# A transformer layer on one core: closing stores taken one to a step, an empty item before the token slots, and a last sum one step later

## The chip, the cores and the metric

The kernel runs on one core of a Trainium2 chip. The metric is the device time of one execution in microseconds (us). A core has TensorE (PE, matrix products, with its weight loads PEld), VectorE (DVE), ScalarE (ACT), GpSimd (POOL) and SyncE (SP). Each engine works through its own instructions in order; SyncE and POOL issue the transfers (DMA) between the chip's main memory (HBM) and the core's memory. Products land in PSUM, of which the kernel holds seven tiles of 512 columns for general use (`unit()`) and an eighth for attention sums.

## What is computed

Four sequences of 1024 tokens with 256 channels go through an attention block and a mixture-of-experts block. All is float32.

```python
x = hidden_states                                   # 4 x 1024 x 256
x = x + layernorm(attention(layernorm(x)))          # 16 heads of 16
    # scores = (q k' + c2p + p2c) / sqrt(48), where c2p and p2c are looked up
    # in products with 128 relative positions by the distance of query and key;
    # out = layernorm(softmax(scores) v Wo + bo + input) * scale + bias
y = layernorm(x)
e = argmax(softmax(y Wr + br))                      # one of 8 experts a token
out = sum over i of (relu((y where e == i) W1[i] + b1[i]) W2[i] + b2[i])
x = x + layernorm(out)
```

A token that is not expert i's enters it as zeros and still receives `relu(b1[i]) W2[i] + b2[i]`. These constants are summed once into one row for each expert, the row of "the other experts" (`drow`, stored to `dh`), and added to the output of the token's own expert.

## The kernel before

**Steps.** The attention works through 128 steps `u` (4 batches x 4 groups of four heads x 8 tiles of 128 queries), and four more that only finish. In step `u`, `tables(u + 4)` multiplies queries and keys with the position tables (L470), copies the result (L478) and stores it to HBM (`shift`, L484). `skewed` reads it back so that each row is shifted by one against the row before it (L497), once as `kpos` and once as `qpos`; it reads for step `u + 3` (`kpos`) and `u + 2` (`qpos`). `mend` (L504, VectorE) adds what lies beyond the table's end: in step `u` for the `kpos` that was issued in step `u - 1`, and for a `qpos` likewise. `turn_x` (L535) brings `kpos` into PSUM, `first_x` (L551) adds the scores, `near_x` (L567, L571) adds `qpos` and takes maxima. `first_y` (L584, L591) does the rest of the keys. A block of four steps later, `turn_near` (L620) and `second` (L642) build the transposed scores, `Exp` (L649) is taken and `attend` (L659) sums. `divide` (L678 to L683) ends a block of four steps, in the first step of the next four.

**Closing work.** When `divide` ends the last group of a batch, it calls `finish` for that half of the batch (first half: steps 32, 64, 96, 128; second half: four steps later). `finish` does nothing at once: it puts items in `queue`. Each step takes items at fixed places (`slot()`, one item each). A step takes three: steps that are not a multiple of four take one ahead of `turn_x`, one ahead of the tables and one at the end, after `first_y`; steps that are a multiple of four take one behind `divide`, one ahead of the tables and one ahead of `first_y`. In the four steps after 127 and in the loop over expert blocks there are five places. The items of a half, with two tile pairs `t` = 0 and 2 each:

- `turn` (L744, L746): transposes; `out_proj` (L754, L758): the product with Wo, the residual, first statistics
- `scale` (L767, L768); then one item of its own, `fetch(b, hf, "x")`, two loads (L727)
- `scaled`, `residual` (POOL, L780), `again`: two further norms; then, for first halves, one item `fetch(b, 1, "xrh")`, two loads (L727) of the second half's residual
- `logits0` (`xn`), `logits` (L806), `logits2` (L817), interleaved: the routing logits
- `choose`: four stores (L785), for each pair one to `x1h` and, but for the last batch, one to `x1a`; then thirteen VectorE instructions (L833 to L843) that find each token's expert and count
- `place` (L849, L850 on TensorE, then VectorE): each token's slot in its expert's list. L849 needs what L840 wrote, L850 what the last L842 wrote
- an item that puts four `scatter` (L862, POOL) in the list `late`, of which `one_late()` takes one in each step

In the step numbers, before the change: `choose` of batch 0's first half stands in the last place of step 38 and `place` in the first of step 39; of its second half in the first and second place of step 46. The other batches follow 32 steps apart each.

**The row of the other experts.** From step 6 on, `others(e)` loads an expert's W2 and `others2(e)` multiplies (L708) and adds to `dsum` (L711, VectorE). In step 29, with the last expert, L714 multiplies with `dsum` right behind L711, L715 adds to `drow` and L716 stores it.

**Expert blocks.** After step 127, 39 blocks of up to 128 tokens are worked through, each with its expert's weights (2 MB). The first 17 hold only tokens of batches 0 to 2 and begin while batch 3 is being finished; their order in `queue` is guarded by `late` being empty. The lists of tokens (`lists`) are first filled with a pad value in step 7 (L226 to L228).

Of the kernel before, what the change touches and what calls it, by code (L numbers as in the profile page):

```python
# [15 lines left out]
P = 128  # L16
B, S, C = 4, 1024, 256
# [7 lines left out]
E, FF = 8, 1024  # L25
# [17 lines left out]
SLOTS = E * NTOK + NTOK  # L43
I32 = mybir.dt.int32
# [4 lines left out]
def tile_layer(  # L49
# [7 lines left out]
    nc = tc.nc  # L57
# [13 lines left out]
    lists = hbm.tile([SLOTS, 1], I32, name="lists")  # L71
# [10 lines left out]
    def rsqrt(agg, n, eps):  # L82

        ve = small.tile([P, NT], F32, name="ve")
        rs = small.tile([P, NT], F32, name="rs")
        nc.vector.tensor_scalar(ve[:, :n], agg[:, :n, 1], eps, None, ALU.add)  # L86
        nc.gpsimd.tensor_tensor(rs[:, :n], ve[:, :n], half[:, :n], ALU.pow)  # L87
        return rs
# [10 lines left out]
    with ExitStack() as ax:  # L99
# [16 lines left out]
        xrh = dram.tile([NTOK, C], F32, name="xrh")  # L116
# [3 lines left out]
        def unit():  # L120
            return p_u.tile([P, 512], F32, name="u")
# [90 lines left out]
        def route_setup():  # L212
            nc.vector.tensor_scalar(ebase, iota, float(E), float(NTOK), ALU.add, ALU.mult)
            nc.gpsimd.affine_select(
                out=before, in_=ones_m, pattern=[[1, P]], compare_op=ALU.is_gt, fill=0.0, base=0, channel_multiplier=-1
            )
            nc.gpsimd.iota(ids, pattern=[[P, B * NT]], base=0, channel_multiplier=1)
            nc.gpsimd.memset(count, 0.0)
            nc.gpsimd.memset(dsum, 0.0)
            for e in range(E):  # L220
                nc.vector.tensor_reduce(four[:, e : e + 1], ident[:, e::HP], AX.X, ALU.add)
            nc.vector.tensor_scalar(num_e, iota, float(E), None, ALU.add)
            nc.gpsimd.iota(steps, pattern=[[1, B * NT]], base=0, channel_multiplier=0, allow_small_or_imprecise_dtypes=True)
            nc.vector.tensor_scalar(behind_t, steps, float(TB), None, ALU.mult)
            nc.vector.tensor_scalar(ahead_t, behind_t, float(TB), None, ALU.add)
            pad = blk_p.tile([P, SLOTS // P], I32, name="pad", bufs=1)  # L226
            nc.gpsimd.memset(pad, NTOK)
            nc.sync.dma_start(out=lists.rearrange("(p n) o -> p (n o)", p=P), in_=pad)  # L228


        def others_tiles(sp):
# [172 lines left out]
        blk_p = ax.enter_context(tc.tile_pool(name="blk", bufs=4))  # L404
# [285 lines left out]
        def others(e):  # L690
            w2 = []
            for n in range(2):
                w2.append(ctp.tile([P, NFC // 2, C], F32, name="w2", tag="o", bufs=2))
                nc.sync.dma_start(
                    out=w2[n], in_=w2_d[e, n * FF // 2 : (n + 1) * FF // 2].rearrange("(f p) c -> p f c", p=P)
                )
            lift = small.tile([P, NFC, HP], F32, name="lift", bufs=2)
            nc.vector.memset(lift, 0.0)
            nc.vector.tensor_copy(lift[:, :, :E], rb[:, e * NFC : (e + 1) * NFC].unsqueeze(2).to_broadcast([P, NFC, E]))
            nc.vector.memset(lift[:, :, e : e + 1], 0.0)  # L700
            begun[e] = w2, lift

        def others2(e):
            w2, lift = begun.pop(e)
            pm = unit()
            for f in range(NFC):
                r = f % 4 * HP
                nc.tensor.matmul(  # L708
                    pm[r : r + HP, :C], lhsT=lift[:, f, :], rhs=w2[f // 4][:, f % 4, :], start=(f < 4), stop=(f >= 4)
                )  # L710
            nc.vector.tensor_tensor(dsum, dsum, pm[:, :C], ALU.add)  # L711
            if e == E - 1:
                pm = unit()
                nc.tensor.matmul(pm[:E, :C], lhsT=four, rhs=dsum, start=True, stop=True)  # L714
                nc.vector.tensor_tensor(drow, drow, pm[:E, :C], ALU.add)  # L715
                nc.sync.dma_start(out=dh, in_=drow)  # L716

        queue, late, fetched = [], [], {}

        def fetch(b, hf, what, places=None):  # L720

            for t in range(0, NT // 2, 2):
                if (b, hf, t, what) not in fetched:
                    w = fetched[b, hf, t, what] = places.pop(0) if places else xin.tile([P, 2, C], F32, name="xt")
                    r0 = b * NT + hf * (NT // 2) + t
                    src = xrh.rearrange("(t p) c -> p t c", p=P) if what == "xrh" else x_d.rearrange("b (t p) c -> p (b t) c", p=P)
                    nc.sync.dma_start(out=w, in_=src[:, r0 : r0 + 2, :])  # L727

        def finish(b, hf):


            HT = NT // 2
            t_0 = hf * HT
            ctx_, o = ctxs[b], ctp.tile([P, HT, C], F32, name="o", bufs=2)
            agg = [small.tile([P, HT, 2], F32, name=f"agg{n}", bufs=2) for n in range(3)]
            rs, keep_ = {}, {}
            pairs = range(0, HT, 2)
# [26 lines left out]
            def scale(t):  # L764
                for n in range(t, t + 2):
                    w = o[:, n, :]
                    nc.vector.scalar_tensor_tensor(w, w, agg[0][:, n, 0:1], obb[:, 1, :], ALU.subtract, ALU.mult)  # L767
                    nc.vector.scalar_tensor_tensor(w, w, rs[0][:, n : n + 1], obb[:, 2, :], ALU.mult, ALU.add)  # L768

            def scaled(t):  # L770
                for n in range(2):
# [10 lines left out]
            def store(t):  # L782
                r0 = (b * NT + t_0 + t) * P
                for d in (x1h, x1a) if b < B - 1 else (x1h,):
                    nc.sync.dma_start(out=d[r0 : r0 + 2 * P, :].rearrange("(t p) c -> p t c", p=P), in_=o[:, t : t + 2, :])  # L785

            def again(t):
                for n in range(2):
                    stats(agg[2][:, t + n, :], o[:, t + n, :])
                if t == HT - 2:  # L790
                    rs[2] = rsqrt(agg[2], HT, 1e-5)

            lg = small.tile([P, HT, E], F32, name="lg", bufs=2)

# [31 lines left out]
            acc = small.tile([P, HT, E], F32, name="acc", bufs=2)  # L826

            def choose():
                for t in pairs:
                    store(t)  # L830

                mx = small.tile([P, HT], F32, name="big")
                nc.vector.tensor_reduce(mx, lg, AX.X, ALU.max)  # L833

                io = iota.unsqueeze(1).to_broadcast([P, HT, E])
                nc.vector.tensor_tensor(lg, lg, mx.unsqueeze(2).to_broadcast([P, HT, E]), ALU.is_equal)
                nc.vector.tensor_tensor(lg, lg, io, ALU.mult)
                ix = small.tile([P, HT], F32, name="ix")
                nc.vector.tensor_reduce(ix, lg, AX.X, ALU.min)
                nc.vector.tensor_tensor(lg, io, ix.unsqueeze(2).to_broadcast([P, HT, E]), ALU.is_equal)  # L840
                for t in range(HT):
                    nc.vector.tensor_copy(acc[:, t, :], count)  # L842
                    nc.vector.tensor_tensor(count, count, lg[:, t, :], ALU.add)  # L843
# [27 lines left out]
            for f in (scale, scaled, residual, again):  # L871
                for t in pairs:
                    queue.append((f, t))
                if f is scale:
                    queue.append((fetch, b, hf, "x"))
                if f is again and hf == 0:
                    queue.append((fetch, b, 1, "xrh"))
            for t in pairs:
                queue.append((logits0, t))
                if t:  # L880
# [1 line left out]
                queue.append((logits, t))  # L882
            queue.append((logits2, HT - 2))
            queue.append((choose,))
            queue.append((place,))
            part = b - (B - 2) if hf and b >= B - 2 else None
            plan = [] if part is None else [(need, part), (spread, part), (slots, part)]
# [217 lines left out]
        def extras(u):  # L1105
            n, i = divmod(u, NT)
            b, g = divmod(n, NG)
            if u >= NU:
                return
            setup_rest(u)  # L1110
            if u % 3 == 0 and 2 <= u // 3 < E + 2:
                others(u // 3 - 2)
            if u % 3 == 2 and 2 <= u // 3 < E + 2:
                others2(u // 3 - 2)
            if g == 0 and i < 4 and b:
                values(b, 2 * i)
            if g == NG - 1 and i == 6:
                fetch(b, 0, "xrh")
            if n + 1 < NU // NT:
                if i == 3:  # L1120
                    project(n + 1, "q", 0)
                    project(n + 1, "k", 0)
                elif i == 5:
                    project(n + 1, "k", 512)
                elif i == 6:
                    project(n + 1, "q", 512)
                if g == NG - 1 and b + 1 < B and 1 <= i < 5:
                    prep2(b + 1, 2 * i - 2)
# [339 lines left out]
```

## Time and profile before

| what | us |
|---|---|
| median of three runs | 2029.2 (2025.56 to 2032.08) |
| the profiled execution, its own time | 2048.3 |
| its span, first to last instruction | 2046.5 |
| mean granted TensorE clock in it | 0.977 |
| HBM traffic | 222 GB/s over the span |

The span in 40 slices of 51 us (a digit is the busy share in tenths; PEclk the granted TensorE clock in tenths):

```profile
PE   7999999999999999999999999999999999899997
DVE  3866676858677668787876677877776784554343
PEclk9899999999999999999999999998999999999999
DMA  8878788877686879776877797767778883999993
```

Slices 1 to 33 are the 128 steps, 34 to 40 the expert blocks. A gap in brackets in an order of time is the idle time ahead of an instruction and what ended it. "Clock 0.50" is a granted clock of half speed, at which matmuls take twice their time.

### The profile page before, as it was taken

To read this page: it belongs to the slowest core of one execution; us is meant where nothing else is said; L and a number is where in the kernel's file an instruction comes from. 1 tells how busy PE (TensorE), PEld (TensorE's weight loads), DVE (VectorE), ACT (ScalarE), POOL (GpSimd) and SP (SyncE) were. 2 spreads that over 40 slices of the span, in tenths; PEclk is the share of its full clock that TensorE was granted. 3 is DMA by queue.
4 is the path that set the end of the run, shared out by engine and by line. 5 is a ranking of instruction groups with operands and counts; after the bars stand their busy time and mean duration, and the time that the engine had idled before them with its cause. 6 is when DMAs were issued, how large, how long until landed. Compare 5 with 4: busy or idle time off the path is not lost.

```text
span 2046.5 us, 43095 instructions
## 1 busy us (share of the span) xinstructions
PE 1947.6 (95%) x15733; PEld 1196.6 (58%) x15733; DVE 1385.9 (68%) x4593; ACT 1006.6 (49%) x2083; POOL 570.2 (28%) x966
## 2 busy tenths in 40 slices
PE   7999999999999999999999999999999999899997
PEld 4555555545555555555555555555545556789996
DVE  3866676858677668787876677877776784554343
ACT  3255556554455555645545555554555544233332
POOL 2121111322122222222222232222222132444442
PEclk9899999999999999999999999998999999999999
DMA  8878788877686879776877797767778883999993
GB/s 257 244 210 238 204 264 237 252 194 200 188 186 191 221 198 258 207 212 178 223 191 200 205 252 210 216 177 184 203 208 218 219 239 121 311 290 344 321 349 109
DMA packets 384013, 456.83 MB, mean 223 GB/s; under 512 B 26243, under 2 KB 371291, under 8 KB 383804
## 3 DMA queue, kind: packets, MB, share of 16 engines
q1 hardware_dynamic: 379036, 444.76, 77.2%
q0 software_dynamic: 4768, 9.33, 1.4%
q8 instruction: 125, 2.05, 0.4%
q14 instruction: 84, 0.69, 0.1%
HBM read 300.07 MB, written 154.89 MB: 222 GB/s over the span
## 4 chain that ended last, share of the span: by engine, by line
PE 75%; DMA 11%; DVE 9%; issue 2%; ACT 1%; POOL 1%; SPq 1%; POOLq 0%; DVEq 0%; ACTq 0%
PE pv L659 10%; PE u L642 9%; PE u L584 8%; PE u L620 7%; PE u L535 7%; PE u L470 7%; PE u L551 6%; PE u L1070 5%; PE u L422 5%; PE u L1056 5%; DMA kpos<-shift 4%; DMA qpos<-shift 3%; DVE mx L591 2%; PE u L754 1%; DVE qpos L504 1%
## 5 line engine op out<-in xcount | busy, mean ns | idle before, releaser
L649 ACT ACTIVATE pt<-u 128x512 f32<-128x512 f32 x1024 | 529.6, 604 | 243.7 <-PE u L642 236.6
L596 POOL TENSOR_SCALAR kept<-kept,m 128x384 f32<-128x384 f32 (+1 forms) x512 | 293.3, 589 | 497.3 <-DVE m L592 334.9
L591 DVE TENSOR_REDUCE mx<-u 128x1 f32<-128x512 f32 x512 | 317.9, 683 | 158.5 <-PE u L584 157.3
L478 ACT COPY stage<-u 128x512 f32<-128x512 f32 x504 | 259.3, 604 | 313.5 <-PE u L470 252.9
L567 DVE CUSTOM_DVE_ANT_0 kept<-u,qpos 128x384 f32<-128x384 f32 (+1 forms) x512 | 264.1, 516 | 153.1 <-PE u L551 152.9
L659 PE MATMUL pv<-pt,v 128*24 128x512 f32 x2048 | 274.9, 608 | 0.0
L620 PEld LDWEIGHTS u<-ident,kept 128*128 128x128 f32 x1408 | 154.1, 142 | 116.5 <-issue 36.2
L620 PE MATMUL u<-ident,kept 128*128 128x128 f32 x1408 | 193.3, 280 | 19.2 <-DVE mx L591 7.1
L535 PE MATMUL u<-ident,kpos 128*128 128x128 f32 x1408 | 191.7, 284 | 6.3 <-DMA kpos<-shift 4.1
L535 PEld LDWEIGHTS u<-ident,kpos 128*128 128x128 f32 x1408 | 157.7, 144 | 66.6 <-DVE mx L591 13.8
L480 POOL COPY ends<-stage 128x8 f32<-128x8 f32 x126 | 26.6, 211 | 593.2 <-ACT stage L478 593.1
L504 DVE SCALAR_TENSOR_TENSOR qpos<-mask,ends,qpos 128x128 f32<-128x128 f32 x448 | 177.9, 457 | 10.4 <-DMA qpos<-shift 10.4
L504 DVE SCALAR_TENSOR_TENSOR kpos<-mask,ends,kpos 128x128 f32<-128x128 f32 x448 | 132.3, 357 | 53.7 <-DMA kpos<-shift 52.9
L571 DVE TENSOR_REDUCE mx<-u 128x1 f32<-128x128 f32 (+1 forms) x512 | 163.3, 319 | 0.0
L584 PE MATMUL u<-k_hi,q 32*128 32x512 f32 (+3 forms) x768 | 154.6, 512 | 5.8 <-ACT pt L649 4.8
L551 PE MATMUL u<-k,q 32*128 32x384 f32 (+2 forms) x1792 | 135.9, 411 | 0.0
L642 PE MATMUL u<-q,k_hi 32*128 32x512 f32 (+3 forms) x1024 | 125.6, 507 | 4.9 <-DVE q L609 2.3
L87 POOL TENSOR_TENSOR rs<-ve,half 128x1 f32<-128x1 f32 (+2 forms) x118 | 82.2, 697 | 171.0 <-DVE ve L86 157.9
L584 PEld LDWEIGHTS u<-k_hi,q 32*128 32x128 f32 x768 | 83.2, 186 | 75.1 <-ACT pt L649 48.7
L470 PE MATMUL u<-tab,q 32*128 32x256 f32 x1024 | 119.3, 432 | 8.0 <-DVE mx L571 6.8
L470 PEld LDWEIGHTS u<-tab,q 32*128 32x128 f32 x1024 | 58.3, 188 | 105.5 <-issue 86.5
L642 PE MATMUL u<-q,k 32*128 32x512 f32 (+3 forms) x1024 | 109.5, 493 | 0.0
(227 smaller groups left out, 2532.7 us busy)
## 6 DMA issues: line engine op xcount, KB each, us to landing
shift<-stage SPq DMA_DIRECT2D x124, 1020.0 KB
kpos<-shift SPq DMA_DIRECT2D x96, 768.0 KB
qpos<-shift SPq DMA_DIRECT2D x96, 768.0 KB
kpos<-in_L_ffn_W_dram SPq DMA_DIRECT2D x40, 512.0 KB
kept<-in_L_ffn_W_dram SPq DMA_DIRECT2D x40, 512.0 KB
pt<-in_L_ffn_W_dram SPq DMA_DIRECT2D x18, 1024.0 KB
kpos<-shift SPq DMA_DIRECT2D x32, 512.0 KB
qpos<-shift SPq DMA_DIRECT2D x32, 512.0 KB
```

What stands on the lines that cost most here:

```text
L470: nc.tensor.matmul(us[h][:, m * (TW + 1) : (m + 1) * (TW + 1)], lhsT=proj[n, src][r : r + HP, ts], rhs=tab[r : r + HP, g, m, :], start=Tru ...
L478: nc.scalar.copy(st[:, h].rearrange("p m w -> p (m w)"), us[h][:, : 2 * (TW + 1)])
L504: nc.vector.scalar_tensor_tensor(w, mask[:, m, :], ends[u][:, m, h : h + 1], w, ALU.mult, ALU.add)
L535: nc.tensor.matmul(us[h][:, (c - a) * P : (c - a + 1) * P], lhsT=near[u - i + c, 1][:, h, at : at + P], rhs=ident, start=(c == a), stop=Fa ...
L567: nc.vector.tensor_tensor_reduce(out=sn[:, h, w0 : w0 + nw], in0=us[h][:, :nw], in1=near[u, 0][:, h, w0 : w0 + nw], scale=1.0, scalar=-3.0 ...
L584: nc.tensor.matmul(us[h][:, at : at + (c1 - c0) * P], lhsT=proj[n, "q"][r : r + HP, i * P : (i + 1) * P], rhs=proj[n, "k_hi" if small_k el ...
L591: nc.vector.tensor_reduce(mx[:, h, 2:3], us[h], AX.X, ALU.max)
L596: nc.gpsimd.tensor_scalar(w, w, m4[:, i % QB, j : j + 1], 1.0, ALU.add, ALU.mult)
L620: nc.tensor.matmul(us[h][:, (t - t0) * P : (t - t0 + 1) * P], lhsT=kept[n * NT + t][:, h, at : at + P], rhs=ident, start=(t == a), stop=Fa ...
L642: nc.tensor.matmul(us[h][:, (f0 - t0) * P : (f1 - t0) * P], lhsT=proj[n, "k_hi" if small_k else "k"][r : r + HP, c * P : (c + 1) * P], rhs ...
L649: nc.scalar.activation(pt[:, h, :], us[h], AF.Exp)
L659: nc.tensor.matmul(pv[h * HP : h * HP + VW, :], lhsT=vals[b][g][:, c, h, :], rhs=pt[:, h, :], start=first, stop=last)
```

## The change

- The two `fetch` items are no longer items of their own: `scale` of the last pair issues the loads of `x`, `again` of the last pair those of `xrh`.
- `choose` no longer issues the stores, but for the very last half: each pair's store is put in `late`, ahead of the scatters, and so is taken by `one_late()`, one pair to a step.
- Between `choose` and `place` stands an empty item (`len` of an empty tuple), again but for the very last half.
- L714 to L716 become a function `others3`, called in step 30 and no longer in step 29.
- The pad tile is half as wide and is stored twice over by one transfer.

With this, a first half has 22 items ahead of its plan instead of 23, and a second half as many as before; in the last batch they are 22 and 21.

```diff
@@ -223,9 +223,11 @@
-            pad = blk_p.tile([P, SLOTS // P], I32, name="pad", bufs=1)
+            pad = blk_p.tile([P, SLOTS // P // 2], I32, name="pad", bufs=1)
             nc.gpsimd.memset(pad, NTOK)
-            nc.sync.dma_start(out=lists.rearrange("(p n) o -> p (n o)", p=P), in_=pad)
+            nc.sync.dma_start(
+                out=lists.rearrange("(p m n) o -> p m (n o)", p=P, m=2), in_=pad.unsqueeze(1).to_broadcast([P, 2, SLOTS // P // 2])
+            )
@@ -709,7 +711,9 @@
             nc.vector.tensor_tensor(dsum, dsum, pm[:, :C], ALU.add)
-            if e == E - 1:
+
+        def others3():
+            if True:
                 pm = unit()
                 nc.tensor.matmul(pm[:E, :C], lhsT=four, rhs=dsum, start=True, stop=True)
                 nc.vector.tensor_tensor(drow, drow, pm[:E, :C], ALU.add)
@@ -766,6 +770,8 @@
                     nc.vector.scalar_tensor_tensor(w, w, rs[0][:, n : n + 1], obb[:, 2, :], ALU.mult, ALU.add)
+                if t == HT - 2:
+                    fetch(b, hf, "x")
@@ -789,6 +795,8 @@
                 if t == HT - 2:
                     rs[2] = rsqrt(agg[2], HT, 1e-5)
+                    if hf == 0:
+                        fetch(b, 1, "xrh")
@@ -826,8 +834,11 @@
             def choose():
-                for t in pairs:
-                    store(t)
+                if (b, hf) == (B - 1, 1):
+                    for t in pairs:
+                        store(t)
+                else:
+                    late.extend((store, t) for t in pairs)
@@ -871,10 +882,6 @@
             for f in (scale, scaled, residual, again):
                 for t in pairs:
                     queue.append((f, t))
-                if f is scale:
-                    queue.append((fetch, b, hf, "x"))
-                if f is again and hf == 0:
-                    queue.append((fetch, b, 1, "xrh"))
@@ -882,6 +889,8 @@
             queue.append((choose,))
+            if (b, hf) != (B - 1, 1):
+                queue.append((len, ()))
             queue.append((place,))
@@ -1110,6 +1119,8 @@
             if u % 3 == 0 and 2 <= u // 3 < E + 2:
                 others(u // 3 - 2)
+            if u == 3 * E + 6:
+                others3()
             if u % 3 == 2 and 2 <= u // 3 < E + 2:
                 others2(u // 3 - 2)
```

## The prediction

> **What bounds the kernel now.** I read the page first, then the waits of TensorE, the clock by stage, the order of time around one closing stage, and the chain.
>
> The page, top and chain:
> ```profile
> span 2046.5 us, 43095 instructions
> PE 1947.6 (95%) x15733; PEld 1196.6 (58%) x15733; DVE 1385.9 (68%) x4593; ACT 1006.6 (49%) x2083; POOL 570.2 (28%) x966
> ...
> PE 75%; DMA 11%; DVE 9%; issue 2%; ACT 1%; POOL 1%; SPq 1%; POOLq 0%; DVEq 0%; ACTq 0%
> ```
> TensorE is the bound; what can be won is its idle time (99 us) and the time it spends at a lower clock. Who ends its idle time up to 1690 us (us in total, times, longest):
> ```profile
> PE u L620 <- DVE o L758: 6.9, 3, 2.7
> ...
> PE u L806 <- DVE xn L91: 4.0, 3, 1.3
> PE u L714 <- DVE dsum L711: 2.8, 1, 2.8
> ```
> and, in the same waits over the whole span, the two matmuls of `place`:
> ```profile
> PE u L850 <- DVE acc L842: 4.6, 3, 1.5
> ...
> PE u L849 <- DVE lg L840: 0.5, 3, 0.2
> ```
> These are the waits that the change can reach: a few per batch, all in closing work. Order of time around `place` of batch 0, first half (step 39):
> ```profile
> 553.31 0.41 PE L849 MATMUL u<-lg,before 128*128 128x32 f32 x2 [0.16 <-DVE lg L840]
> ...
> 555.24 0.64 PE L850 MATMUL u<-acc,ones_m 128*128 128x32 f32 x2 [1.52 <-DVE acc L842]
> ```
> The stages around it (length, busy us by engine, then granted clock, DMA share, GB/s):
> ```profile
> 552.00:555.05 3.05, 1.56 (x11) 0.61 (x10) 2.74 (x11) 2.57 (x5) 2.27 (x4) 1.00 1.04 212
> 555.05:558.50 3.45, 3.26 (x18) 2.85 (x22) 2.01 (x10) 0.18 (x1) 0.00 (x0) 0.50 1.03 328
> 558.50:561.90 3.40, 3.40 (x24) 1.00 (x22) 2.22 (x10) 0.00 (x0) 0.00 (x0) 0.50 0.74 258
> 561.90:565.00 3.10, 3.10 (x35) 1.49 (x33) 1.62 (x7) 2.14 (x5) 0.04 (x1) 1.00 0.00 0
> ```
> A wait of 1.69 us is followed by 6.8 us at clock 0.50, which costs half of itself again, 3.4 us. Stages of 2 us over the whole span show the same behind `place` of batch 2 (1384 to 1392), none behind that of batch 1, and one of half the length (1.7 us lost) behind L714 (428 to 434).
>
> The chain in order of time (start, us):
> ```profile
> 565.54 11.94 DMA kpos<-shift
> ...
> 596.99 13.54 DMA kpos<-shift
> ...
> 979.20 10.77 DMA kpos<-shift
> ...
> 1006.77 12.12 DMA kpos<-shift
> ```
> So the other weak place is the read `kpos<-shift`, which `mend` (L504) needs one step after its issue. Where the next step is one of eight (40, 48, ...), the distance is shortest and VectorE waits. Step 40:
> ```profile
> 577.58 1.14 DVE L504 SCALAR_TENSOR_TENSOR kpos<-mask,ends,kpos 128x128 f32<-128x128 f32 x4 [3.64 <-DMA kpos<-shift]
> ...
> 579.38 1.11 PE L620 MATMUL u<-ident,kept 128*128 128x128 f32 x4 [2.70 <-DVE o L758]
> ```
> L758 stands behind L504 on VectorE and holds a PSUM tile that L620 wants. Clock 0.50 follows from 578 to 586.
>
> **The change part by part, in us of the profiled execution (gain positive).**
>
> *`others3` a step later.* L714 waited 2.81 us at 425.0 and 1.7 us were lost at clock 0.50. In step 30 its operand is a step old. Gain 4.5; 0 if TensorE only meets the next late read sooner, so 0 to 4.5. L714 itself (0.59 us) and the store of `dh` stay.
>
> *The empty item before `place`.* `choose` takes 2.8 to 3.6 us on VectorE; with an item between, `place` comes half a step later. Three of the six closings before the last batch wait (first halves): 3 x 1.69 = 5.1, and two clock losses of 3.4: 11.9. The second halves have `choose` in the first slot and `place` in the second, and no gap; the first halves now get `choose` in that first slot, where VectorE idled 3.68 us at 543.22 for L551. I cost that at nothing; without this cover it would be 3 x 2.8. What is late next: with the wait gone, `mend` in step 39 comes earlier. In batch 1, which has no clock loss to blur it, 11.3 us lie between issue (965.77) and `mend` (977.11); 9.6 will be left. Reads that VectorE was seen waiting for took 8.8 to 12.8 us from issue to `mend` where no closing load or store stood near. So 0 to 3.2 us of VectorE wait per batch. At 610.56 a VectorE wait of 2.93 became 1.46 on TensorE; at 1018.91 1.77 became 0.33. I take 1.0 for each: 3.0 back (bounds 0 and 9.6). Net 8.9.
>
> *Stores one to a step.* Before, SyncE issues four stores (1 MB) in a row at 550.91 to 554.7, and the DMA share is 0.04 at 561 to 564: the burst had drained before the read at 565.54, so it was not what made that read late, and spreading it gains nothing there. After, the first pair goes out behind the reads of step 38, the second right behind those of step 39, whose `kpos` is the tight one. What half a megabyte behind a read costs: the two loads of `x` (L727) stand behind the read at 596.99. Compared with the read two steps earlier it took 13.54 against 11.94, in batch 1 12.12 against 10.77, in batch 2 11.48 against 11.85: +1.6, +1.4, -0.4, mean 0.9. Against that, the items are also earlier: TensorE now does L754 x16 in step 40 ahead of the contested L620 instead of L744 x4 and L754 x8, 1.89 - 0.66 = 1.2 us more work to cover the wait. Net 0.3 less wait per batch, 0.9 gain. Bounds: all three waits and their clock losses go (6.9 + 6.8 = 13.7 gain), or each grows by 1.6 and batch 1 gets its clock loss too (4.8 + 3.4 = 8.2 loss). The second half's later pair falls behind `kpos` of step 46, whose `mend` comes 9.1 us after issue without a wait: 0, at worst 3 x 1.6 = 4.8 loss.
>
> [...]
>
> *The loads of `x` joined to `scale`.* In second halves they move from behind the reads of step 41 to ahead of its table store, where the DMA share is 0.02 (594 to 597). The wait at 610.56 (1.46 on TensorE, 1.7 of clock) can go; I take half, 1.6; bounds 0 and 3.5. In first halves their place among SyncE's DMAs is the same.
>
> *Everything else moves by one or two slots.* The wait of L806 for `xn` (3 x 1.32, second halves, both items in one step of four with little between) vanishes there and arises in the first halves, which take that place: 0, bounds 4 either way. `choose` of second halves now stands in the second slot, where VectorE idles 2.05 us ahead of L591 (549.19), less than 2.8: L591 0.8 us late; I charge 0.5 x 3 = 1.5 loss, bounds 0 and 4.1 (3 x 0.8 and one clock loss). POOL's scatter, which waited 7.12 us for the one before it at 577.58, comes a step later; POOL is 28% busy: 0. `pad` halves one memset in step 7 under TensorE work: 0.
>
> *The tail (after 1690).* Closing items of batch 3 run between expert blocks, with waits of 0.8 to 4.2 us on TensorE (L1044 7.0 in total, L806 5.2). Two empty items go and the order against `center` shifts. I see no sign; 0, bounds 7 either way.
>
> Sum: 4.5 + 8.9 + 0.9 + 1.6 - 1.5 = 14.4 us. The execution took 2048.3 us, 1.8 outside its span; the median of the runs shown is 2029.2, 19 us less, so I take the gain off the median: **2014.8 us**.
>
> **The rivals.**
> 1. *The waits go, the slow clock doesn't.* The low-clock stages all last a multiple of 3.4 us, and batch 1 shows the same 1.69 us wait without one. If they simply arise at other gaps, only waits count: 2.8 + 5.1 - 3.0 + 0.9 + 0.7 - 1.5 = 5.0, time 2024.2. Against it: both long ones follow directly on a wait of `place`. [...]
> 2. *The stores meet the reads* (slower). In steps 39, 40 and 47 of three batches `kpos` has half a megabyte behind it. If every one costs 1.6 us that reach TensorE and a short clock loss (1.7): 9 x 3.3 = 29.8 against 18.0 gained (4.5 + 11.9 + 1.6): 2029.2 + 11.8 = 2041.0. It decides from 2.0 us of lost TensorE time at each of the nine. For it: step 40 has no slack. Against: batch 1's read of step 38 had a whole megabyte behind it and was there in 11.3 us.
> 3. *The tables set the pace.* Each step moves 2.6 MB of `shift` (1020 + 768 + 768 KB); at the 243 to 265 GB/s of 567 to 573 that is 9.9 to 10.8 us of a step of 11 to 13. Every gain at `place` then returns at the next `mend`, and 0 to 4.5 stays: about 2027. Against: 561 to 564 is idle.
> 4. *The wait of step 40 goes as well:* 12.8 more, 2002.0.
>
> **How the numbers follow.** Chances: forecast 0.48 (own range 2005 to 2023), rival 1 0.20, rival 2 0.14, rival 3 0.10, rival 4 0.08. Below 0.3% (6.1 us) a measurement of this kernel can't tell a difference from none. Faster (under 2023.1): 0.46 + 0.08 + half of rival 1, 0.09 = 0.63. Slower (over 2035.3): rival 2 and a bad tail, 0.15. The rest, 0.22, is the same. Range 2003 to 2037: it leaves out half of rival 4 and much of rival 2.
>
> **What would show it.** Right: no wait of L714, L849 or L850 on TensorE before 1690; clock 1.00 behind both; L806 waiting about 1.3 us in first halves. `mend` in steps 39 and 40 shows the price: over 3.6 us of wait there speaks for rival 2, none for rival 4; as many low-clock stages as before (16 and the end) for rival 1. I am wrong if closings lose as much TensorE time as before.

## The result, and the profile after

| | before | after |
|---|---|---|
| median of 20 runs each, us | 2031.5 (2023.02 to 2038.98) | 2026.07 (2019.25 to 2031.63) |
| ratio after to before, 95% interval | | 0.9968 [0.9955, 0.9981] |
| profiled execution, its own time, us | 2048.3 | 2021.1 |
| its span, us, and mean granted clock | 2046.5, 0.977 | 2019.2, 0.985 |

The change gains 6.5 us by the ratio (0.32%, 3.9 to 9.1 by the interval), where 14.4 were forecast. The two profiled executions differ by 27 us, four times that. The profiled execution of before took longer than any of the 20 timed runs, so the pair of profiles can't be subtracted line by line. What can be compared is which instructions wait, and where.

The top of the page of after:

```profile
span 2019.2 us, 43078 instructions
PE 1929.4 (96%) x15733; PEld 1183.0 (59%) x15733; DVE 1384.7 (69%) x4593; ACT 1007.1 (50%) x2083; POOL 570.3 (28%) x966
```

TensorE is idle for 2019.2 - 1929.4 = 89.8 us instead of 98.9. The chain of waits names only some 13% of this span and is not read here. Who ended TensorE's idle time up to 1690 us (total, times, longest; code lines stand further down than before, by two at the tables and up to eleven at `place`: L472 is the old L470, L622 the old L620, L814 the old L806, L860 and L861 the old L849 and L850):

```profile
PE u L472 <- DVE mx L573: 13.4, 15, 1.6
PE u L622 <- DVE mx L593: 9.0, 8, 2.4
...
PE u L814 <- DVE xn L91: 4.0, 3, 1.3
...
PE u L472 <- DVE v L454: 2.7, 3, 0.9
...
PE u L622 <- DVE o L762: 0.7, 3, 0.2
```

L714 and both matmuls of `place` are no longer among them. L814 waits as long as before, but now in first halves (509.83, 920.84, 1327.17). The wait of L620 for `o`, 6.9 before, is down to 0.7, but the same tiles are now waited for under another name, as step 40 below shows. And the matmuls of the tables, L472, wait for the maxima of `near_x` and, three times 0.9 us, for `v`. `place` of batch 0's first half in the order of time, with no bracket and so no idle time ahead:

```profile
540.70 0.41 PE L860 MATMUL u<-lg,before 128*128 128x32 f32 x2
540.94 0.39 PE L861 MATMUL u<-acc,ones_m 128*128 128x32 f32 x2
```

And step 40, first VectorE's `mend`, then TensorE's L622:

```profile
567.36 1.14 DVE L506 SCALAR_TENSOR_TENSOR qpos<-mask,ends,qpos 128x128 f32<-128x128 f32 x4 [1.55 <-DMA qpos<-shift]
```
```profile
571.06 0.55 PE L622 MATMUL u<-ident,kept 128*128 128x128 f32 x3 [2.11 <-DVE mx L593]
```

The late read is now `qpos`; behind it VectorE has four instructions of `scale` (1.9 us) ahead of the maxima that TensorE waits for, 2.11 us. In batch 1, where no read is late, 0.46 is left, in batch 2 1.39. The stages around (length, busy us by engine TensorE, weight load, VectorE, ScalarE, POOL, then granted clock, DMA share, GB/s):

```profile
535.00:560.00 25.00, 25.00 (x201) 13.02 (x194) 19.70 (x68) 14.16 (x27) 5.86 (x11) 1.00 0.72 201
560.00:575.00 15.00, 12.64 (x112) 7.77 (x114) 12.15 (x33) 6.83 (x14) 3.00 (x6) 1.00 0.82 222
```

So `place` costs neither a wait nor clock any more, as forecast. Where the gain went is to be seen behind this, in the second half of the same batch. VectorE, POOL and TensorE from the end of step 41 to the tables of step 42, in order of time:

```profile
583.81 2.40 POOL L598 TENSOR_SCALAR kept<-kept,m 128x384 f32<-128x384 f32 x4 [2.81 <-PE u L644]
...
584.72 0.26 DVE L86 TENSOR_SCALAR ve<-agg 128x4 f32<-128x4 f32 x1
...
586.17 1.07 POOL L87 TENSOR_TENSOR rs<-ve,half 128x4 f32<-128x4 f32 x1
...
587.28 0.74 DVE L91 TENSOR_SCALAR o<-o,agg,rs 128x256 f32<-128x256 f32 x2 [0.68 <-POOL rs L87]
587.93 0.55 DVE L569 CUSTOM_DVE_ANT_0 kept<-u,qpos 128x384 f32<-128x384 f32 x1
...
588.84 0.45 PE L472 MATMUL u<-tab,q 32*128 32x256 f32 x1 [1.12 <-DVE mx L573]
```

The closing item here is a norm. POOL takes its power (L87) only after four instructions of its own (L598), so VectorE stands 0.68 us and then norms for 0.74. Behind that on VectorE's queue stands `near_x` (L569), which frees the PSUM tile that the next table matmul wants: TensorE waits 1.12 us. One step later, in step 43, it is the statistics of the next norm that stand there:

```profile
599.23 0.42 DVE L79 BATCH_NORM_STATS2 st<-o 128x6 f32<-128x256 f32 x1
...
600.42 0.17 DVE L86 TENSOR_SCALAR ve<-agg 128x4 f32<-128x4 f32 x1
600.50 0.55 DVE L569 CUSTOM_DVE_ANT_0 kept<-u,qpos 128x384 f32<-128x384 f32 x1
...
601.40 0.45 PE L472 MATMUL u<-tab,q 32*128 32x256 f32 x1 [1.60 <-DVE mx L573]
```

The same 1.12 and 1.60 come in batches 1 and 2 (998.22, 1010.78; 1406.76, 1419.32), as do 0.89 (490.60, 899.97, 1307.93) behind `v` in the first halves, 3.6 us a batch in all. Before, second halves had 0.50 (619.80) and twice 2.0 us (1028.16, 1447.06) at this line.

### The profile page after: what moved, and what is told of

It is laid out like the page before. It is cut to its first block, busy times and chain, and to the rows that moved or that the text cites. A ratio compares the mean times of both kernels' runs of the same rounds, so it can differ in the third digit from the quotient of the medians.

```text
span 2019.2 us, 43078 instructions
## 1 busy us (share of the span) xinstructions
PE 1929.4 (96%) x15733; PEld 1183.0 (59%) x15733; DVE 1384.7 (69%) x4593; ACT 1007.1 (50%) x2083; POOL 570.3 (28%) x966
## 5 line engine op out<-in xcount | busy, mean ns | idle before, releaser
L598 POOL TENSOR_SCALAR kept<-kept,m 128x384 f32<-128x384 f32 (+1 forms) x512 | 293.6, 589 | 507.6 <-DVE m L594 350.1
L569 DVE CUSTOM_DVE_ANT_0 kept<-u,qpos 128x384 f32<-128x384 f32 (+1 forms) x512 | 264.5, 517 | 144.1 <-PE u L553 144.0
L622 PEld LDWEIGHTS u<-ident,kept 128*128 128x128 f32 x1408 | 153.2, 141 | 109.6 <-issue 29.2
L622 PE MATMUL u<-ident,kept 128*128 128x128 f32 x1408 | 192.5, 279 | 12.6 <-DVE mx L593 9.0
L537 PEld LDWEIGHTS u<-ident,kpos 128*128 128x128 f32 x1408 | 153.6, 141 | 69.8 <-DVE mx L593 15.2
L472 PE MATMUL u<-tab,q 32*128 32x256 f32 x1024 | 120.4, 426 | 17.2 <-DVE mx L573 13.4
L87 POOL TENSOR_TENSOR rs<-ve,half 128x1 f32<-128x1 f32 (+2 forms) x118 | 82.4, 699 | 164.0 <-DVE ve L86 152.9
L472 PEld LDWEIGHTS u<-tab,q 32*128 32x128 f32 x1024 | 57.9, 183 | 114.0 <-issue 97.4
L644 PE MATMUL u<-q,k_hi 32*128 32x512 f32 (+3 forms) x1024 | 121.2, 496 | 2.6 <-DVE q L611 2.1
```

Source lines behind the costliest of these rows:

```text
L472: nc.tensor.matmul(us[h][:, m * (TW + 1) : (m + 1) * (TW + 1)], lhsT=proj[n, src][r : r + HP, ts], rhs=tab[r : r + HP, g, m, :], start=Tru ...
L537: nc.tensor.matmul(us[h][:, (c - a) * P : (c - a + 1) * P], lhsT=near[u - i + c, 1][:, h, at : at + P], rhs=ident, start=(c == a), stop=Fa ...
L569: nc.vector.tensor_tensor_reduce(out=sn[:, h, w0 : w0 + nw], in0=us[h][:, :nw], in1=near[u, 0][:, h, w0 : w0 + nw], scale=1.0, scalar=-3.0 ...
L598: nc.gpsimd.tensor_scalar(w, w, m4[:, i % QB, j : j + 1], 1.0, ALU.add, ALU.mult)
L622: nc.tensor.matmul(us[h][:, (t - t0) * P : (t - t0 + 1) * P], lhsT=kept[n * NT + t][:, h, at : at + P], rhs=ident, start=(t == a), stop=Fa ...
L644: nc.tensor.matmul(us[h][:, (f0 - t0) * P : (f1 - t0) * P], lhsT=proj[n, "k_hi" if small_k else "k"][r : r + HP, c * P : (c + 1) * P], rhs ...
```

## The experiments

Two pairs of theories were set against each other. On the clock: A, the waits went as forecast, but the clock losses in the forecast belong to one profiled execution with an unusually low clock; B, each clock loss belongs to its wait and goes with it. On what took gain back: C, the `fetch` items, though they do no work on an engine, kept the items behind them at good places, and joining them costs; D, the later stores meet the reads of `shift`. C was split later: C1, the place in the queue counts; C2, the time at which the loads are issued.

Each kernel was timed against the kernel before in five rounds, in three sessions on three chips; a session's kernel before is the same runs for all its kernels. Sessions shift both: before had a median of 2031.5 in the first measurement and of 2025.9 to 2026.1 in these three, so gains are read within a session. To separate clock from the rest, each run's span times its granted clock is taken as its time at full clock, and (1 - clock) x span as what the lower clock took. This rests on the matmuls: the eight of L754 took 3.78 us at clock 0.50 (581.59 in the profiled execution of before) and 1.89 us at 1.00 (986.79 there). The columns "at full clock" and "of clock" are the gains in the means of these two over the session's kernel before (1990.7, 1991.1, 1989.8 and 34.1, 33.6, 34.5 us). The time at full clock scatters by 1.4 to 3.5 us from run to run (standard deviation), less than the time itself. "Idle" is span less busy time of TensorE in the profiled execution.

| session | kernel | median us | ratio to before [95%] | gain at full clock | gain of clock | idle |
|---|---|---|---|---|---|---|
| 1 | before, run as one of the others | 2022.27 | 0.9984 [0.9963, 1.0006] | 1.2 | 2.8 | 88.8 |
| 1 | the change | 2017.65 | 0.9955 [0.9934, 0.9977] | 5.3 | 3.4 | 88.1 |
| 1 | `others3` alone | 2017.87 | 0.9958 [0.9935, 0.998] | 4.0 | 3.7 | 88.5 |
| 1 | empty item alone | 2008.1 | 0.9905 [0.9872, 0.9938] | 12.7 | 5.7 | 75.3 |
| 2 | `others3` and empty item | 2003.62 | 0.9893 [0.9865, 0.9922] | 16.9 | 5.9 | 69.5 |
| 2 | the change, `fetch` items kept | 2009.15 | 0.9926 [0.9895, 0.9958] | 12.6 | 4.6 | 75.3 |
| 2 | the change, four stores in `choose` | 2020.87 | 0.9968 [0.9948, 0.9989] | 3.2 | 2.6 | 89.1 |
| 2 | `fetch` items joined, alone | 2041.74 | 1.0081 [1.0049, 1.0112] | -8.7 | -6.2 | 99.4 |
| 3 | the change, empty items for `fetch` | 2012.32 | 0.9936 [0.9916, 0.9955] | 8.6 | 5.0 | 73.4 |
| 3 | `others3`, empty item, `x` joined | 2029.38 | 1.0014 [0.9997, 1.0031] | -1.2 | -1.7 | 86.6 |
| 3 | `others3`, empty item, `xrh` joined | 2011.62 | 0.9928 [0.9912, 0.9944] | 7.7 | 6.4 | 85.7 |
| 3 | stores alone | 2025.77 | 0.9998 [0.9981, 1.0014] | 2.4 | -2.3 | 88.5 |

The first row is what a kernel without a change gives: gains of 1 at full clock and 3 of clock mean nothing.

**The kernel before, once more, unchanged.**

> The kernel before, unchanged, for the clock of many executions and a second trace. Theory A (clock losses aren't tied to the closing waits): its executions have a mean granted clock like those of the changed kernel, 0.982 to 0.984 (clock loss 32 to 37 us), and the execution profiled first, with 0.977, was one of the worst; in the second trace the waits of L714, L850 and L758 are there again at the same sizes, within 0.3 us, but the low-clock stages stand behind other waits. Theory B (the losses follow the waits, as the prediction's sum had it): the executions have 0.976 to 0.979, the low-clock stages behind L714 and L850 of batches 0 and 2 are there again, and the missing 8 us of gain were given back elsewhere.

Its second profiled execution had a span of 2014.1 at clock 0.987, 32 us less than the first. Its waits up to 1690, beside those the prediction showed:

```profile
PE u L470 <- DVE mx L571: 6.8, 7, 2.0
...
PE u L850 <- DVE acc L842: 4.5, 3, 1.5
PE u L806 <- DVE xn L91: 4.0, 3, 1.3
...
PE u L620 <- DVE o L758: 3.4, 3, 1.4
...
PE u L714 <- DVE dsum L711: 2.8, 1, 2.8
```

The waits for `mx`, `acc`, `xn` and `dsum`, which follow from the order of instructions, repeat to 0.1 us (6.8, 4.6, 4.0 and 2.8 in the first). The one that hangs on a DMA, L620, halves (6.9 to 3.4). The lower clock cost 28.2 us instead of 48.8 (half the length of the trace's low-clock stages). Behind L850 of batch 0 (1.51 us, up to 546.53) and L714 came one such stage of 3.4 us each, behind L850 of batches 1 and 2 none. At `place` this speaks for A: one execution does not give the price of these waits in clock, and the first had drawn much of it. At L714 it speaks for B: a stage of 3.41 us begins behind this wait in all five traces here that have it.

**The changed kernel, once more, and `others3` alone.** The second puts back everything but this:

```diff
-            if e == E - 1:
+        def others3():
...
+            if u == 3 * E + 6:
+                others3()
```

> The changed kernel again, beside the kernel before on the same chip, for a second trace. Theory A: 0.995 to 0.999 of the time before, idle time of TensorE the same as in the first trace within 2 us, the low-clock stages at other places than there. Theory B: the same places, and the same 31 us lost.

> Only the sum of the other experts' row a step later. The wait of 2.81 us before L714 goes in both. Theory A: 2 to 3 us gained, ratio 0.9985 to 0.999. Theory B: 4.5 us, ratio 0.9978.

The change repeats (0.9955 against 0.9968, the intervals overlap), with 13.2 us of waits of L472 for the maxima and 2.7 for `v`. `others3` alone comes to 0.9958. So this one part measures as much as the whole change. In its trace L714 no longer waits, and the 4.5 for `acc` and the 4.0 for `xn` stand as before. At full clock it gains 4.0, or 2.8 against the unchanged kernel's 1.2, around its wait of 2.81 us. How much clock comes with it can't be told from the runs: by the medians it is 4.4 us shorter than the unchanged kernel and 8.1 than the session's other runs of it.

**The empty item alone, and with `others3`.**

```diff
             queue.append((choose,))
+            if (b, hf) != (B - 1, 1):
+                queue.append((len, ()))
             queue.append((place,))
```

> Only the empty item between choose and place, nothing else. The waits of L849 and L850 in the first halves (3 x 1.69 us) go in both. Theory A: 2 to 5 us gained, ratio 0.9975 to 0.999. Theory B: 8.9 us, ratio 0.9956. If mend of the next step is too early for its read, VectorE waits for kpos there and less than 2 us is left.

> Two parts, the sum a step later and the empty item; stores and fetch items as before. With e6, e7 and the changed kernel it makes a square over (stores, fetch items). Theory C (joining the fetch items to other items costs what the rest gains, since each closing item then stands one or two places earlier, where its operands aren't ready): 2003 to 2006 us, span less clock loss about 1974.5 (1990.5 before, less 3.7 and 12.5 as the two parts alone gave). Theory D (the late stores cost it): the same for this kernel.

The empty item alone gains more than the whole change: 0.9905, 12.7 us at full clock and 5.7 of clock, above both expectations. With `others3` it is 0.9893, the shortest time of all. The waits of the second:

```profile
PE u L470 <- DVE mx L571: 9.7, 10, 1.8
...
PE u L620 <- DVE mx L591: 4.1, 6, 1.8
...
PE u L808 <- DVE xn L91: 2.0, 4, 1.0
```

There is no wait for `acc` or `o` among them any more, and those of L808 are 0.34 us each in the first three batches, where they were 1.32. VectorE still waits for the late read at step 40, in batch 0 and likewise in the other two:

```profile
563.72 1.14 DVE L504 SCALAR_TENSOR_TENSOR qpos<-mask,ends,qpos 128x128 f32<-128x128 f32 x4 [3.08 <-DMA qpos<-shift]
```

TensorE no longer waits there, since the product with Wo now stands behind the L620 that waited. In this kernel every second half begins one place later than before, since it stands in the queue behind a first half of 24 items instead of 23. In the change a first half has 22, and every second half begins one place earlier. The two joined loads took away two places where the empty item had given one. Not all of the gain lies there: with the empty item alone TensorE idles 13.5 us less than in the second profiled execution of before, 9.1 of it up to the last L551 (1643.5 here, 1648.0 there) and 4.4 in the tail behind it.

**The four corners: stores early or late, `fetch` kept or joined** (with `others3` and the empty item throughout; two corners are the change and the kernel just shown). The first keeps the items of `fetch` (and the full pad tile), the second the four stores in `choose`:

```diff
-                if t == HT - 2:
-                    fetch(b, hf, "x")
...
+                if f is scale:
+                    queue.append((fetch, b, hf, "x"))
+                if f is again and hf == 0:
+                    queue.append((fetch, b, 1, "xrh"))
```
```diff
-                if (b, hf) == (B - 1, 1):
-                    for t in pairs:
-                        store(t)
-                else:
-                    late.extend((store, t) for t in pairs)
+                for t in pairs:
+                    store(t)
```

> The changed kernel with the two fetch items kept as items of their own; stores late, empty item and later sum as in the change. Theory C: as fast as e5, span less clock loss 1973 to 1977, about 10 us under the changed kernel. Theory D: near the changed kernel, 1984 to 1988.

> The changed kernel with the four stores issued by choose as before; fetch items joined, empty item and later sum as in the change. Theory C: like the changed kernel, span less clock loss 1984 to 1988, with the waits of L806 for xn (3 x 1.3) and of the table matmuls (3 x 0.9, 1.1 and 1.6) still there. Theory D: 1973 to 1977.

| gain at full clock, us | `fetch` kept | `fetch` joined |
|---|---|---|
| four stores in `choose` | 16.9 | 3.2 |
| one to a step | 12.6 | 5.3 (session 1) |

Joining costs 13.7 with the stores early, in one session and with intervals of the ratio far apart (0.9893 [0.9865, 0.9922] against 0.9968 [0.9948, 0.9989]), and 7.3 with the stores late. That is C. Both kernels with `fetch` joined also have the narrow pad tile, those with `fetch` kept the full one; what that can hide is bounded below. The stores have no sign of their own: 4.3 dearer late where `fetch` is kept, 2.1 cheaper where it is joined. D falls. In the second kernel's trace, with the stores early, the waits of L472 and L814 are those of the change (13.8, 2.7 and 4.0), so they don't come from the stores.

**`fetch` joined alone.**

> Only the fetch items joined to scale and again. It moves place ahead of the point where it waits (second slot of step 38, as in second halves), so the wait of L850 goes without the empty item. Theory C: it gains those 5 us and pays the new waits; span less clock loss 1986 to 1992 (1990.5 before). Theory D: 1980 or less, as the joined loads cost nothing.

Alone it makes the kernel slower by 0.81%, some 16 us: 8.7 at full clock and 6.2 of clock. TensorE's waits:

```profile
PE u L810 <- DVE xn L91: 11.3, 6, 2.4
PE u L470 <- DVE mx L571: 9.9, 12, 1.3
PE u L620 <- DVE mx L591: 9.6, 7, 2.6
...
PE u L854 <- DVE acc L846: 3.7, 3, 1.2
```

At full clock it was expected at 1986 to 1992 us and came to 1999.8. The wait for `acc` has left the first halves, as expected, but has come up in the second ones, three times 1.22. The wait for `xn` is there in first and second halves now, with 1.32 and 2.44. One of the latter, from the end of step 42 into step 43:

```profile
602.01 0.27 DVE L86 TENSOR_SCALAR ve<-agg 128x4 f32<-128x4 f32 x1
602.18 1.73 DVE L504 SCALAR_TENSOR_TENSOR qpos<-mask,ends,qpos 128x128 f32<-128x128 f32 x4
603.48 1.08 POOL L87 TENSOR_TENSOR rs<-ve,half 128x4 f32<-128x4 f32 x1
604.60 0.73 DVE L91 TENSOR_SCALAR xn<-o,agg,rs 128x256 f32<-128x256 f32 x2 [0.68 <-POOL rs L87]
605.15 0.67 PE L810 MATMUL u<-ident,xn 128*128 128x128 f32 x4 [2.45 <-DVE xn L91]
```

`again` ends with the variance (L86); `logits0` (L91) needs its power from POOL (L87) and is itself what the matmul wants. No `fetch` item ever stood between these two in second halves. They have only come three places earlier: before, `again` was the last item of step 43 and `logits0` the first of step 44, which as a multiple of four takes it behind `divide`, and TensorE waited 1.32 us. Now `logits0` is the first item of step 43, ahead of `turn_x` and with only a `mend` behind `again`, and the three engines stand in a chain.

**Place or load (C1 or C2).** The loads stay joined as in the change, empty items stand where `fetch` stood:

```diff
                 queue.append((f, t))
+                if f is scale or (f is again and hf == 0):
+                    queue.append((len, ()))
```

> The changed kernel, loads still issued by scale and again, but with an empty item where each of the two fetch items stood. Theory C1 (what counts is the spacing of the items, the place that each gets in its step): as e6, span less clock loss 1977 to 1981, 2007 to 2012 us; the waits of L806 for xn and of the table matmuls behind the norms go. Theory C2 (the moved issue of the loads costs it): as the changed kernel, 1985 to 1989.

```profile
PE u L472 <- DVE mx L573: 9.9, 10, 2.0
PE u L622 <- DVE mx L593: 7.4, 5, 2.6
...
PE u L814 <- DVE xn L91: 1.0, 3, 0.3
```

The waits for `xn`, but for 0.33 each, and the three of 0.89 are gone, and of 1.12 and 1.60 one of 1.8 to 2.0 a batch is left, which the kernels that keep `fetch` have too (596.8 to 598.6 in that with `others3` and the empty item). The gain at full clock is 8.6, between 5.3 for the change and 12.6 with `fetch` kept; the ratio, 0.9936, is close to the 0.9926 of the latter, with overlapping intervals. C1 holds for the named waits: they go without a load being moved. Whether the remaining 4 us at full clock belong to the loads' issue (C2), to the pad tile, whose half width this kernel has and that one has not, or to the sessions, is open.

**Which of the two.** From `others3` and the empty item, one load joined at a time.

> e5 with only the loads of x joined to scale (both halves). By the places: in first halves the four norm and residual items come one place earlier, in second halves everything two. Theory C1: it pays the waits of the table matmuls (0.9 per batch in first halves, 1.1 and 1.6 in second ones, less the 1.8 that e5 has there): 3 to 6 us over e5's 1974.2 in span less clock loss.

> e5 with only the loads of xrh joined to again (first halves). Logits and all after come one place earlier. Theory C1: 3 to 7 us over e5; the wait of L806 for xn (1.3) comes in one half of each batch, where both logits items fall into one step of four. If C1 is right, e10 and e11 add up to about the 11 us between e5 and the changed kernel, less what the stores take.

Against 16.9 for the kernel that they start from, the first loses 18.1 at full clock and 7.6 of clock, the second 9.2 and nothing. More was lost than expected in both (3 to 6 and 3 to 7), and their sum is twice what both cost together (13.7). The waits of the first:

```profile
PE u L470 <- DVE mx L571: 14.1, 13, 2.4
...
PE u L620 <- DVE o L760: 5.1, 3, 2.6
...
PE u L470 <- DVE v L452: 2.7, 3, 0.9
```

In first halves the waits of the tables are those of the change, 0.89 for `v` among them; in second halves they are 0.91 and 2.41 instead of 1.12 and 1.60. The second kernel has 8.8 for maxima at the tables and none for `v`, so the waits of the tables come with the item of `x`; it has 5.8 for `xn` instead. The wait for `o` of before is back in both (5.1 and 4.9), since with 23 items the second half begins where it began before. So a place is not a price that can be added: each kernel puts all later items into other slots. TensorE idles 17.1 us more in the first than in the kernel without the joined load: 12.0 up to the last L551 (1660.9 here, 1640.2 there), as much as the waits for `o` and of the tables have grown, and 5.1 in the tail, which no run took apart.

**Stores alone.**

> Only the stores one to a step, on the kernel before. Where the fetch items were kept they cost 4 us (e6 against e5), where they were joined nothing or a small gain (changed kernel against e7). Rival: half a megabyte behind a read lengthens it, so VectorE waits longer for kpos in step 40 and 47: 1993 to 1998 in span less clock loss (1990.5 before). Else, no cost of their own: 1989 to 1992.

0.9998 [0.9981, 1.0014]: no effect that can be measured. The waits for `acc` (4.5) and `xn` (4.0) stand unchanged in its trace.

## Why the prediction was right in its sign and wrong in its size

- **`others3`, 4.5:** right. The wait of 2.81 went. Alone the kernel gains 2.8 to 4.0 at full clock. The 1.7 of clock can't be read from the runs, but the traces bear it out: a stage of 3.41 us behind L714 in five of five that have the wait, none there where it is gone.
- **The empty item, 8.9:** right at `place`, too small as a whole. Alone it gives 12.7 us at full clock and 5.7 of clock. The sum moved only `place` and `choose`. It missed that the whole second half, which stands in the queue behind them, comes one place later and loses its waits for `xn` (3 x 1.32 become 3 x 0.34) and `o` (3.4 in the second profiled execution of before). The 3.0 us charged back at `mend` of step 39 didn't come: VectorE has no wait there. And the tail, which the sum put at nothing, idles 4.4 us less in the trace.
- **Stores, 0.9:** no effect that could be measured, inside the bounds: the stores alone came to 0.9998 [0.9981, 1.0014]. The differences of +1.6, +1.4 and -0.4 between three pairs of reads were no measure of it.
- **"The loads of `x` joined to `scale`", +1.6, and "Everything else moves by one or two slots", 0 and -1.5 for `choose`:** here the prediction failed. Joining the loads measures -7 to -14 us at full clock instead. The sum took a joined load as a DMA that is issued elsewhere, and asked of the moved items only what covers their own instructions. It named the move of L806's wait from second to first halves, and that came to the digit (3 x 1.32). It did not ask which instructions the moved items would stand in front of: norms and statistics ahead of `near_x` and, through its PSUM tile, ahead of TensorE's tables. At L472 the waits for maxima grew from 6.8 (second profiled execution of before) to 13.4, and 2.7 for `v` came in: 9.3 us. What the change took away in waits is 7.8: 5.0 of `place` and 2.8 of L714. The wait at step 40 went on under another name: 3.4 for `o` in that execution of before, 0.7 for `o` and 4.0 for maxima (2.11, 0.46, 1.39) in after. So TensorE's idle time is what it was, 88.8 us in that execution of before, 89.8 and 88.1 in the two of after, although the waits of `place` and of L714 are gone.
- **Clock losses:** 9.4 of the 14.4 (1.7 + 2 x 3.4 + 1.7/2) were lower clock, taken from one execution at 0.977; the runs of before in the three sessions have 0.983 on average. Behind L850 the four traces that have its wait of 1.51 us show eight stages after twelve waits, 37.5 us long in all: 4.7 us lost a kernel, not 6.8. And the sum has no loss at waits that stay or are new: in the two traces of after three stages each follow waits of step 40, of the tables or for `v`, 5.1 and 6.8 us lost. The change gains 3.4 us of clock in the runs, little more than the 2.8 of the unchanged kernel beside it.
- **The rivals.** The first (2024.2: the waits go, the slow clock stays) came closest in its number, but by luck: it had nothing of the new waits, and it let no clock loss go with a wait, where the one of L714 does. Whether clock is won in step with idle time is open: 5.9 us of it were gained at 69.5 us idle (`others3` and empty item), 6.4 at 85.7 (`xrh` joined). The second, stores against reads (9 x 3.3 is 29.7, not 29.8), falls with the square of four and the stores alone. The third, tables that set the pace, falls too: the same steps can be run 17 us shorter at full clock. The fourth, that step 40's wait goes as well (2002.0), is false for the change; with the empty item it does go, and that kernel with `others3` takes 2003.62.
- **Signs named beforehand:** no wait of L714, L849 or L850, clock 1.00 around `place`, L806 in the first halves: all came. `mend` waited for no read in step 39, and 1.55, 0 and 0.80 us in step 40, which settles none of the rivals. The number of low-clock stages (16 and the end before, 12 and the end after) told nothing, since the unchanged kernel had 10 and the end in its second profiled execution.

The parts alone, each from its ratio to a before of 2026 us, give +8.5 for `others3`, +19.2 for the empty item, +0.4 for the stores and -16.4 for `fetch`: 11.7, beside 6.5 and 9.1 for the whole. The first two without the others are the best version that was run: 2003.62 us, 0.9893 [0.9865, 0.9922].

## What to carry to other kernels

In a queue that is served at fixed places, an item without work is still distance: before one is joined or added, count the shift of the whole queue behind it (here two places less and one more) and list what each later item will then stand in front of on its engine, above all where a norm passes from VectorE to POOL and back (VectorE stood 0.68 us for it here, and TensorE up to 2.44 us with `fetch` joined alone). Four waits that follow from the order of instructions repeated to 0.1 us in two executions of before (6.8 and 6.8, 4.6 and 4.5, 4.0 and 4.0, 2.8 and 2.8) and could be read from one; the clock losses (48.8 and 28.2) and the wait that hangs on a DMA (6.9 and 3.4) did not repeat, and such are priced over several.

## What the hardware showed that was not expected

Which waits cost clock can be counted over the fourteen traces. A stage of half clock is counted here when it begins during the wait or within 3 us of its end.

| TensorE's wait | idle time close together, us | half clock follows |
|---|---|---|
| `place` in second halves, `fetch` joined alone, 1.22 | 1.22 | 0 of 3 |
| for `xn`, 1.32 | 1.32 | 0 of 27 |
| tables for `v`, 0.89, with 0.61 close behind | 1.5 | 6 of 15 |
| L850 for `acc`, 1.51, with 0.16 just ahead | 1.7 | 8 of 12 |
| for `xn`, `fetch` joined alone, 2.44 | 2.44 | 3 of 3 |
| L714 for `dsum`, 2.81 | 2.81 | 5 of 5 |

In these rows half clock followed the more often, the more idle time came together: 0 of 30 up to 1.32 us, 14 of 27 at 1.5 and 1.7, 8 of 8 at 2.44 and 2.81. A single wait still does not tell. In the trace of after, the 0.89 and 0.61 us at 899 to 901 (batch 1) are followed by half clock, and 2.11 us at 569 to 571 (batch 0) by none (columns as above):

```profile
570.00:572.00 2.00, 0.94 (x12) 0.66 (x12) 2.00 (x4) 0.00 (x0) 0.00 (x0) 1.00 1.08 229
572.00:574.00 2.00, 1.99 (x28) 1.59 (x27) 1.93 (x6) 1.89 (x4) 0.79 (x2) 1.00 1.02 291
...
899.00:901.00 2.00, 0.79 (x10) 0.34 (x6) 2.00 (x12) 0.00 (x0) 0.45 (x1) 1.00 0.62 231
901.00:903.00 2.00, 1.71 (x10) 1.09 (x10) 2.00 (x10) 0.53 (x2) 0.81 (x1) 0.62 0.00 2
```

The same wait in batches 0 and 2 had none behind it. All low-clock stages but the last of a trace are, in all fourteen traces, 3.41, 6.83, 10.24 or 13.65 us long, multiples of 3.41. What sets this length, and why the same wait is followed by half clock in one batch and not in another, no run here shows. Idle time of 1.5 us in two pieces was followed by it six times of fifteen. The same program lost 48.8 us to the clock in one execution and 28.2 in another.
